# Rotation tables with the norm weights in them, and the rms factor on ScalarE, in a sparse and local attention layer

## The chip, the core and the metric

The kernel runs on one core of a Trainium2 chip. The core has five engines with instruction queues of their own: TensorE (PE in the profile; PEld is its weight load), VectorE (DVE), ScalarE (ACT), GpSimd (POOL) and SyncE (SP, which here only issues DMAs). They meet through semaphores. SBUF is the working memory with 128 partitions, PSUM is where TensorE accumulates. The metric is the device time of one execution in microseconds, lower is better.

## The reference

Four sequences of 1024 tokens with 512 features pass through a layer norm, and then the sum of three things is returned: the input, an attention block and a small product of 8-bit rounded operands. The attention has 16 heads of 128. Queries and local keys are projected, normalized by their root mean square, multiplied by a norm weight for each feature, and half of their features are rotated by an angle that depends on the token:

```python
def rmsnorm(x, w):
    return x * jax.lax.rsqrt(jnp.mean(x * x, axis=-1, keepdims=True) + EPS) * w
...
def apply_rope(x, pos):
    ...
    x1, x2, rest = (x[..., :half], x[..., half:ROPE_DIM], x[..., ROPE_DIM:])
    return jnp.concatenate([x1 * cos - x2 * sin, x1 * sin + x2 * cos, rest], axis=-1)
...
q = apply_rope(rmsnorm(q, qn_w), pos)
...
lk = apply_rope(rmsnorm((hidden_states @ Wlk + blk).reshape(Bq, Sq, NH, D).transpose(0, 2, 1, 3), kn_w), pos)
```

Here `half` is 32 and `ROPE_DIM` 64, so features 64 to 127 are only scaled. Each query then attends in two ways, and the two contexts are averaged: over its own and the previous window of 128 tokens with `lk`, and over the eight best of the compressed entries, one entry for four tokens. The output projection `Wo` follows.

## The kernel before

A chunk is 128 tokens: there are 32, numbered t, eight in each sequence; c is the place of a chunk in its sequence. A unit is one chunk and two heads, so a chunk has eight units u, and there are 256 units n. The number of compressed entries that a chunk sees grows with c, so steps with a large c have wider tiles on TensorE, VectorE and ScalarE.

The order of work is written out by hand: instructions stand on each engine in the order in which the program emits them, and each engine runs its own in that order. The loop over steps s (from L789) works on several units at once. In step s it emits, in this order:

- scores of unit s on TensorE (`scores`, L570 to L581: keys of the previous window, of the own window, compressed keys, mask);
- `keep_context` of unit s - 2 on ScalarE (L733), which moves a finished context out of PSUM;
- `weigh` of unit s: masks, maxima and the eight best on VectorE (L603 to L609), exponentials on ScalarE (L610, L618);
- `queries` of unit s + 2 on TensorE (L443, L444): one PSUM tile `qp` of 128 x 512 with two query heads and two local key heads;
- `settle` of unit s on VectorE (L625 to L636);
- `squares` of unit s + 2 on ScalarE (L294), and `spread` on GpSimd (L288, L289), which makes the factor `r` = 1/rms for each of the four heads;
- `settle_window` of unit s on ScalarE (L641), `to_output` of unit s - 2 on TensorE (L751);
- `turn` of unit s: the probabilities are transposed in 32 x 32 blocks on VectorE (L659) and written to DRAM by SP (L667);
- `values_of` of unit s + 1 on TensorE (L535);
- `normalize` of unit s + 2, the subject of the change;
- `values` of unit s - 1 on TensorE (L718);
- `fetch` of unit s on SP (L701), which reads the probabilities back with the blocks exchanged and so must wait until they have landed;
- `turn_keys` and `fetch_keys` of unit s + 2: block transposes on VectorE (L510, L513) into `thb`, four DMAs to DRAM (L518), two back (L528) into `qT` and `lkT`, all on SP;
- `keep_values` of unit s + 1 on ScalarE (L547).

So keys normalized in step s are used by the scores at the head of step s + 2. Units 0 to 7, and the last one's probabilities, are transposed on TensorE instead (`turn_keys_here`, L488). Beside this run two generators, one that prepares the chunk after next (layer norm and compressed entries) and `chunk_eight`, which rounds the chunk for the 8-bit product with four long GpSimd instructions (L266 to L272) in steps u = 3 and 4, and adds its result in u = 5 (L429).

`normalize` does this for one unit: four VectorE instructions (L465), one for each head, read 128 x 128 of `qp` out of PSUM and multiply by `r` and by the norm weight into `th`. Then `rotate` multiplies the first 64 features of all four heads by the sine on GpSimd (L307, into `rb`) and by the cosine on VectorE (L308, into a spare part of `thb`), and VectorE forms the difference (L309) and the sum (L310) in `th`. `rotate` also serves the compressed keys (`rb_e`, `ra_e`). `th`, `thb` and `rb` have one buffer each; `qp` has two. The table `cs` holds the 32 cosines and 32 sines of each token of a chunk and is loaded two chunks ahead at the end of step u = 6.

Of the kernel before, what the change touches and what calls it, by code (L numbers as in the profile page):

```python
# [12 lines left out]
F32 = mybir.dt.float32  # L13
# [3 lines left out]
ALU = mybir.AluOpType  # L17
AX = mybir.AxisListType

P = 128  # L20
D = 128
RATIO = 4
ROPE = 64
# [15 lines left out]
def kernel(  # L39
# [256 lines left out]
    def rotate(th, cs, nh, a, name):  # L296

        p = th.shape[0]
        a = a.rearrange("p (h t f) -> p h t f", h=nh, t=2)
        bb = work.tile([P, 4, 2, HALF], F32, tag="ropeb", name=f"rb_{name}", bufs=1)  # L300
        bb = bb[:p, 0:nh]
        x12 = th[:, :, 0:ROPE].rearrange("p h (t f) -> p h t f", t=2)

        def wide(v):
            return v.unsqueeze(1).unsqueeze(1).to_broadcast([p, nh, 2, HALF])

        nc.gpsimd.tensor_tensor(bb, x12, wide(cs[:, HALF:ROPE]), ALU.mult)  # L307
        nc.vector.tensor_tensor(a, x12, wide(cs[:, 0:HALF]), ALU.mult)  # L308
        nc.vector.tensor_tensor(x12[:, :, 0, :], a[:, :, 0, :], bb[:, :, 1, :], ALU.subtract)  # L309
        nc.vector.tensor_tensor(x12[:, :, 1, :], a[:, :, 1, :], bb[:, :, 0, :], ALU.add)  # L310
# [144 lines left out]
    def spread(n):  # L455
        w = units[n]
        w["r"] = rstd_of(w["ss"], 4, 1.0 / D, EPS_RMS, f"r_{n}")

    def normalize(n):
        t, u = place(n)  # L460
        w = units[n]
        qp, r = w.pop("qp"), w["r"]
        th = work.tile([P, 4, D], F32, tag="th", name=f"th_{n}", bufs=1)
        for i in range(4):
            nc.vector.scalar_tensor_tensor(  # L465
                th[:, i, :],
                qp[:, ts(i, D)],
                r[:, i : i + 1],
                norm_w[:, i // 2, :],
                ALU.mult,  # L470
                ALU.mult,
            )
        thb = work.tile([P, NB, 2, 2 * BLK], F32, tag="thb", name=f"thb_{n}", bufs=1)
        spare = thb.rearrange("p b t x -> p (b t x)")[:, 0 : 4 * ROPE]
        rotate(th, angles[t][0], 4, spare, f"{n}")
        w["th"], w["thb"] = th, thb

    def by_dma(n):
# [297 lines left out]
    def for_unit(n, *todo):  # L776
        if 0 <= n < NN:
            for f, *more in todo:
                f(n, *more)
# [9 lines left out]
    for s in range(-2, NN + 2):  # L789
# [7 lines left out]
        if u == 4 and 0 <= t and t + 2 < NT:  # L797
            load_x(t + 2, "norm")

        for_unit(s, (scores, 0), (scores, 1))  # L800
        for_unit(s - 2, (keep_context,))
        for_unit(s, (weigh, 0), (weigh, 1))
# [95 lines left out]
```

## Time and profile before

| What | Value |
| --- | --- |
| Median of three runs | 2824.78 us (2822.69 to 2830.02) |
| Profiled execution | 2828.88 us, of which the span from first to last instruction is 2827.2 us |
| Granted TensorE clock in it, mean | 0.997 |
| TensorE busy | 2775.0 us, 98% of the span |
| VectorE busy | 2277.4 us, 81% |
| ScalarE busy | 1302.9 us, 46% |
| GpSimd busy | 818.0 us, 29% |
| L465, 1024 instructions | 282.9 us, 338 ns each |
| L307, 256 | 247.4 us, 966 ns each |
| L308, 256 | 108.8 us, 425 ns each |
| L309 and L310, 256 each | 87.1 and 72.5 us, 340 and 283 ns |
| L733 (PSUM to SBUF, 128 x 128), 512 | 160.4 us, 364 ns each |
| L641 at 128 x 128, 64 | 22.2 us, 393 ns each |

Busy times of one engine's instructions overlap a little when they follow each other, so that four L465 of 338 ns each take 1.12 us together. A busy share says how much an engine had to do, not whether anyone waited for it; for that the starts of its instructions and the table of waits are read. In a timeline, each line gives the start in us from the beginning of the span, the duration, the engine and line, the operation with output and inputs, and in brackets how long the engine was idle before it and what ended that.

### The profile page before, as it was taken

How to read it: one execution, taken by the hardware profiler on the slowest of the kernel's cores; microseconds unless marked ns; L12 is line 12 of the kernel's file. 1: busy time of each engine (PE TensorE's matmuls, PEld its weight loads, DVE VectorE, ACT ScalarE, POOL GpSimd, SP SyncE). 2: the span in 40 equal slices, each digit the busy share in tenths (PEclk: the TensorE clock that was granted, in tenths of full speed). 3: DMA queues.
4: the chain of work that ended last, by engine and by line, in shares of the span. 5: the costliest groups of instructions: out<-in, count | busy, mean ns of one | idle time of the engine just before them, and what ended most of it. 6: DMA issues, size and time to landing. Idle time of an engine off the chain costs nothing. (4 is left out here: it accounts for less than half of the span.)

```text
span 2827.2 us, 48528 instructions
## 1 busy us (share of the span) xinstructions
PE 2775.0 (98%) x12770; PEld 1879.6 (66%) x12969; DVE 2277.4 (81%) x9132; ACT 1302.9 (46%) x5075; POOL 818.0 (29%) x1161
## 2 busy tenths in 40 slices
PE   7999999999999999999999999999999999999998
PEld 4666666666666666666666666666666666666666
DVE  5778888888777888888877788888887777888886
ACT  3444444444444444444444444444444444444443
POOL 3433222222233332232223233222223222322222
PEclk9999999999999999999999999999999999999999
DMA  7344445555444445555544444555554444455553
GB/s 224 93 140 133 137 143 151 147 153 146 133 128 133 138 134 149 148 152 151 148 129 123 137 134 138 150 153 147 149 146 124 134 131 131 136 152 151 149 149 116
DMA packets 620851, 399.85 MB, mean 141 GB/s; under 512 B 306880, under 2 KB 573984, under 8 KB 620576
## 3 DMA queue, kind: packets, MB, share of 16 engines
q1 hardware_dynamic: 608352, 383.18, 47.8%
q10 hardware_dynamic: 12224, 13.56, 1.5%
q8 instruction: 105, 1.72, 0.3%
q14 instruction: 170, 1.39, 0.2%
HBM read 212.53 MB, written 184.03 MB: 140 GB/s over the span
## 5 line engine op out<-in xcount | busy, mean ns | idle before, releaser
L443 PE MATMUL qp<-wqk,xnT 128*128 128x512 f32 x2048 | 944.6, 604 | 4.1 <-DMA scales<-in_L_ffn_scale_dram 3.1
L443 PEld LDWEIGHTS qp<-wqk,xnT 128*128 128x128 f32 x2048 | 370.1, 191 | 383.9 <-issue 370.3
L610 ACT ACTIVATE prob<-sc,neg 128x256 f32<-128x256 f32 (+1 forms) x512 | 236.1, 461 | 786.4 <-DVE taken L609 772.5
L535 PEld LDWEIGHTS vp<-wlv,xnT 128*128 128x128 f32 x2048 | 391.1, 191 | 170.4 <-issue 109.5
L535 PE MATMUL vp<-wlv,xnT 128*128 128x256 f32 x2048 | 488.6, 382 | 6.2 <-DVE lkT L495 2.9
L751 PE MATMUL op<-wo,cT 128*128 128x512 f32 x1024 | 488.0, 599 | 6.0 <-ACT cT L733 1.5
L659 DVE STREAM_TRANSPOSE probB<-prob 128x512 f32<-128x512 f32 (+2 forms) x494 | 282.9, 610 | 79.4 <-ACT prob L641 75.8
L294 ACT ACTIVATE junk<-qp 128x128 bf16<-128x128 f32 x1024 | 284.2, 278 | 100.0 <-remote 56.6
L307 POOL TENSOR_TENSOR rb<-th,cs 128x256 f32<-128x256 f32 x256 | 247.4, 966 | 276.5 <-DVE th L465 276.5
L465 DVE SCALAR_TENSOR_TENSOR th<-qp,r,norm_w 128x128 f32<-128x128 f32 x1024 | 282.9, 338 | 45.1 <-POOL r L289 44.9
L751 PEld LDWEIGHTS op<-wo,cT 128*128 128x128 f32 x1024 | 186.5, 190 | 179.2 <-issue 115.9
L547 ACT COPY lv<-vp 128x256 f32<-128x256 f32 x256 | 95.4, 373 | 449.5 <-PE cp L718 393.5
L288 POOL TENSOR_SCALAR r<-ss 128x4 f32<-128x4 f32 x256 | 49.8, 195 | 862.8 <-ACT junk L294 856.4
L718 PE MATMUL cp<-probT,lv 128*128 128x128 f32 x1920 | 298.3, 275 | 0.7 <-DMA probT<-pr 0.7
L718 PEld LDWEIGHTS cp<-probT,lv 128*128 128x128 f32 x1920 | 275.3, 192 | 14.3 <-PE vp L535 1.1
L289 POOL TENSOR_TENSOR r<-r,nhalf 128x4 f32<-128x4 f32 x256 | 259.9, 1015 | 21.4
L718 PE MATMUL cp<-probT,cv 128*128 128x128 f32 x1536 | 255.6, 275 | 0.0
L580 PE MATMUL sc<-ckT,qT 128*128 128x96 f32 (+7 forms) x1024 | 226.2, 303 | 0.0
L641 ACT ACTIVATE prob<-prob,tot 128x256 f32<-128x256 f32 (+1 forms) x512 | 223.0, 484 | 2.1 <-DVE tot L635 2.0
L309 DVE TENSOR_TENSOR th<-thb,rb 128x128 f32<-128x128 f32 x256 | 87.1, 340 | 158.9 <-POOL rb L307 158.9
L577 PE MATMUL sc<-lkT,qT 128*128 128x128 f32 x1024 | 209.7, 287 | 5.4 <-DMA lkT<-qk 3.9
L718 PEld LDWEIGHTS cp<-probT,cv 128*128 128x128 f32 x1536 | 213.2, 192 | 0.0
(123 smaller groups left out, 4003.8 us busy)
## 6 DMA issues: line engine op xcount, KB each, us to landing
pr<-probB SPq DMA_DIRECT2D x127, 512.0 KB, 2.6
probT<-pr SPq DMA_DIRECT2D x508, 128.0 KB, 2.9
qk<-thb SPq DMA_DIRECT2D x992, 64.0 KB, 2.0
pr<-probB SPq DMA_DIRECT2D x96, 384.0 KB, 2.3
probT<-pr SPq DMA_DIRECT2D x384, 96.0 KB, 2.5
qT<-qk SPq DMA_DIRECT2D x248, 128.0 KB, 2.3
lkT<-qk SPq DMA_DIRECT2D x248, 128.0 KB, 2.5
x_norm<-_attn_hidden_states_dram SPq DMA_DIRECT2D x32, 256.0 KB, 3.1
```

The source lines that it names most:

```text
L289: nc.gpsimd.tensor_tensor(r, r, nhalf[: ss.shape[0], 0:n], ALU.pow)
L294: nc.scalar.activation(junk[: src.shape[0]], src, AF.Square, accum_out=acc)
L307: nc.gpsimd.tensor_tensor(bb, x12, wide(cs[:, HALF:ROPE]), ALU.mult)
L443: nc.tensor.matmul(qp, xnT[:, k, :], wqk_sb[u][:, k, :], start=(k == 0), stop=False)
L465: nc.vector.scalar_tensor_tensor(th[:, i, :], qp[:, ts(i, D)], r[:, i : i + 1], norm_w[:, i // 2, :], ALU.mult, ALU.mult,)
L535: nc.tensor.matmul(vp[:, 0:256], xnT[:, k, :], wlv_sb[u][:, k, :], start=(k == 0), stop=(k == KK - 1),)
L580: nc.tensor.matmul(sc[:, spa], q, ckT[:, 0:m], start=True, stop=False)
L610: nc.scalar.activation(prob[:, loc], sc[:, loc], AF.Exp, bias=neg[:, 0:1], scale=-1.0, accum_out=tot[:, 0:1],)
L641: nc.scalar.mul(prob[:, loc], prob[:, loc], tot[:, 0:1])
L659: nc.vector.transpose(pb[:, :, ds(h * g, g), :], prob[:, parts[0] * P : (parts[-1] + 1) * P].rearrange("p (g b i) -> p b g i", b=NB, i=BLK),)
L718: nc.tensor.matmul(blocks(cp[:, h, :]), v, probT[:, :, h * len(parts) + i - parts[0], :], start=(i == parts[0]), stop=(i == parts[-1]),)
L751: nc.tensor.matmul(op, cT[:, h, :], wo_sb[u][:, h, :], start=(u == 0 and h == 0), stop=(u == NU - 1 and h == 1),)
```

## The change

Per chunk, GpSimd now builds two tables out of the norm weights and the chunk's angles: `cos` (128 x 2 x 128: weight times cosine for the rotated features, the bare weight for the rest) and `sin` (128 x 2 x 2 x 32: weight times sine, with the sign in it). They are built at the head of step u = 6 for the next chunk, with one buffer each, and the sines in `cs` are negated in place for it. Per unit, ScalarE multiplies each head of `qp` by its `r` into `thb`, GpSimd multiplies the two exchanged halves by `sin` in two instructions, and VectorE multiplies everything by `cos` in one and adds the two in another. The compressed keys keep `rotate`.

```diff
+    def make_tables(t):
+        cs, _ = angles[t]
+        cos = work.tile([P, 2, D], F32, tag="cos", name=f"cos_{t}", bufs=1)
+        sin = work.tile([P, 2, 2, HALF], F32, tag="sin", name=f"sin_{t}", bufs=1)
+        halves = norm_w[:, :, 0:ROPE].rearrange("p g (t f) -> p g t f", t=2)
...
+        nc.gpsimd.tensor_tensor(
+            cos[:, :, 0:ROPE].rearrange("p g (t f) -> p g t f", t=2),
+            halves,
+            wide(cs[:, 0:HALF], 2, 2),
+            ALU.mult,
+        )
+        nc.gpsimd.tensor_copy(cos[:, :, ROPE:D], norm_w[:, :, ROPE:D])
+        nc.gpsimd.tensor_tensor(
+            sin[:, :, 1, :], halves[:, :, 0, :], wide(cs[:, HALF:ROPE], 2), ALU.mult
+        )
+        nc.gpsimd.tensor_scalar(cs[:, HALF:ROPE], cs[:, HALF:ROPE], -1.0, None, ALU.mult)
+        nc.gpsimd.tensor_tensor(
+            sin[:, :, 0, :], halves[:, :, 1, :], wide(cs[:, HALF:ROPE], 2), ALU.mult
+        )
+        tables[t] = cos, sin
+
     def normalize(n):
         t, u = place(n)
         w = units[n]
         qp, r = w.pop("qp"), w["r"]
+        cos, sin = tables[t]
         th = work.tile([P, 4, D], F32, tag="th", name=f"th_{n}", bufs=1)
+        thb = work.tile([P, NB, 2, 2 * BLK], F32, tag="thb", name=f"thb_{n}", bufs=1)
+        xr = thb.rearrange("p b t x -> p (b t x)")
         for i in range(4):
-            nc.vector.scalar_tensor_tensor(
-                th[:, i, :],
-                qp[:, ts(i, D)],
-                r[:, i : i + 1],
-                norm_w[:, i // 2, :],
+            nc.scalar.mul(xr[:, ts(i, D)], qp[:, ts(i, D)], r[:, i : i + 1])
+        xr = xr.rearrange("p (g h d) -> p g h d", g=2, h=2)
+        rb = work.tile([P, 2, 2, 2, HALF], F32, tag="ropeb", name=f"rb_{n}", bufs=1)
...
+        for i in range(2):
+            nc.gpsimd.tensor_tensor(
+                rb[:, :, :, i, :],
+                xr[:, :, :, ds((1 - i) * HALF, HALF)],
+                heads_of(sin[:, :, i, :]),
                 ALU.mult,
-                ALU.mult,
-            )
-        thb = work.tile([P, NB, 2, 2 * BLK], F32, tag="thb", name=f"thb_{n}", bufs=1)
-        spare = thb.rearrange("p b t x -> p (b t x)")[:, 0 : 4 * ROPE]
-        rotate(th, angles[t][0], 4, spare, f"{n}")
+            )
+        all_ = th.rearrange("p (g h) d -> p g h d", g=2)
+        nc.vector.tensor_tensor(all_, xr, heads_of(cos), ALU.mult)
+        turned = th[:, :, 0:ROPE]
+        nc.vector.tensor_tensor(
+            turned, turned, rb.rearrange("p g h t f -> p (g h) (t f)"), ALU.add
+        )
         w["th"], w["thb"] = th, thb
...
+        if u == 6 and t + 1 < NT:
+            make_tables(t + 1)
         for_unit(s, (scores, 0), (scores, 1))
```

More of the change, by code (lines that the diff above doesn't have):

```diff
@@ L457, in spread, with wide @@
         w["r"] = rstd_of(w["ss"], 4, 1.0 / D, EPS_RMS, f"r_{n}")
+    tables = {}
+    def make_tables(t):
[3 more added lines that the diff above has]
+        halves = norm_w[:, :, 0:ROPE].rearrange("p g (t f) -> p g t f", t=2)
+        def wide(v, *ones):
+            for _ in ones:
+                v = v.unsqueeze(1)
+            return v.to_broadcast([P, *ones, HALF])
+        nc.gpsimd.tensor_tensor(
[13 more added lines that the diff above has]
+        tables[t] = cos, sin
     def normalize(n):
@@ L462, in normalize, with heads_of @@
         qp, r = w.pop("qp"), w["r"]
+        cos, sin = tables[t]
         th = work.tile([P, 4, D], F32, tag="th", name=f"th_{n}", bufs=1)
+        thb = work.tile([P, NB, 2, 2 * BLK], F32, tag="thb", name=f"thb_{n}", bufs=1)
+        xr = thb.rearrange("p b t x -> p (b t x)")
         for i in range(4):
-            nc.vector.scalar_tensor_tensor(
-                th[:, i, :],
-                qp[:, ts(i, D)],
-                r[:, i : i + 1],
-                norm_w[:, i // 2, :],
-                ALU.mult,
+            nc.scalar.mul(xr[:, ts(i, D)], qp[:, ts(i, D)], r[:, i : i + 1])
+        xr = xr.rearrange("p (g h d) -> p g h d", g=2, h=2)
+        rb = work.tile([P, 2, 2, 2, HALF], F32, tag="ropeb", name=f"rb_{n}", bufs=1)
+        def heads_of(v):
+            return v.unsqueeze(2).to_broadcast([P, 2, 2, v.shape[-1]])
+        for i in range(2):
[3 more added lines that the diff above has]
+                heads_of(sin[:, :, i, :]),
                 ALU.mult,
             )
-        thb = work.tile([P, NB, 2, 2 * BLK], F32, tag="thb", name=f"thb_{n}", bufs=1)
-        spare = thb.rearrange("p b t x -> p (b t x)")[:, 0 : 4 * ROPE]
-        rotate(th, angles[t][0], 4, spare, f"{n}")
+        all_ = th.rearrange("p (g h) d -> p g h d", g=2)
[4 more added lines that the diff above has]
+        )
         w["th"], w["thb"] = th, thb
```

## The prediction

> **What bounds the kernel now.** I read the page's shares first, then the spacing of TensorE's matmuls, then who TensorE waited for, and last the path from `r` to the keys, which is the only path through the edited code that TensorE waits on.
>
> ```profile
> span 2827.2 us, 48528 instructions
> ...
> PE 2775.0 (98%) x12770; PEld 1879.6 (66%) x12969; DVE 2277.4 (81%) x9132; ACT 1302.9 (46%) x5075; POOL 818.0 (29%) x1161
> ```
>
> 98% on PE can mislead, because matmul ends are modelled. So I took the starts of the matmul records instead. In the timeline a 512-column float32 pass of the query product (L443) starts 429 ns after the one before, a 256-column pass (L535) 216 ns, a 128-column pass of L718 112 ns, without gaps. The time from one unit's first query matmul to the next is a fixed pattern: for chunks 2, 10, 18 and 26 (the same place c = 2 in each batch) the eight steps read 9.96, 10.38, 10.01, 10.45, 11.75, 10.01, 10.76, 10.87 us, and all but one of the 32 agree within 0.1 us. An engine that waits on others does not repeat like that. Adding only the starts that come over 150 ns later than the usual spacing gives 42.2 us lost: about 23 us before 81 us, 7 us after 2800 us, the other 12 in some 25 short waits between. That is all a lighter VectorE could return.
>
> In the table of waits the ones that hold TensorE's matmuls (waiter, awaited, us in total, times, longest) are small:
>
> ```profile
> PE sc L577 <- DMA lkT<-qk: 3.9, 8, 1.2
> ...
> PE tq L488 <- DVE th L310: 3.2, 1, 3.2
> ...
> PE vp L535 <- DVE lkT L495: 2.9, 2, 2.1
> ...
> PE sc L570 <- DMA qT<-qk: 2.0, 3, 1.4
> ```
>
> Only the first and the last recur: keys that come back late from DRAM. The chain of waits at the end runs through VectorE, but that is where a chain goes when TensorE has no gap to follow; its step length in chunk 31 (10.81 to 11.29 us) is TensorE's own.
>
> The path of one unit's keys, from the timeline (start, us, engine, line; unit 137):
>
> ```profile
> 1507.00 1.02 POOL L289 TENSOR_TENSOR r<-r,nhalf 128x4 f32<-128x4 f32 x1
> ...
> 1508.05 1.12 DVE L465 SCALAR_TENSOR_TENSOR th<-qp,r,norm_w 128x128 f32<-128x128 f32 x4 [0.98 <-POOL r L289]
> ...
> 1509.21 0.42 DVE L308 TENSOR_TENSOR thb<-th,cs 128x256 f32<-128x256 f32 x1
> ...
> 1509.26 0.97 POOL L307 TENSOR_TENSOR rb<-th,cs 128x256 f32<-128x256 f32 x1 [1.24 <-DVE th L465]
> ...
> 1510.26 0.29 DVE L309 TENSOR_TENSOR th<-thb,rb 128x128 f32<-128x128 f32 x1 [0.62 <-POOL rb L307]
> ...
> 1510.47 0.28 DVE L310 TENSOR_TENSOR th<-thb,rb 128x128 f32<-128x128 f32 x1
> ...
> 1510.79 0.45 DVE L510 STREAM_TRANSPOSE thb<-th 128x256 f32<-128x256 f32 x1
> ...
> 1511.15 0.40 DVE L513 STREAM_TRANSPOSE thb<-th 128x256 f32<-128x256 f32 x1
> ...
> 1511.75 1.82 SPq L518 DMA_DIRECT2D qk<-thb  x4
> ...
> 1515.06 0.38 SPq L528 DMA_DIRECT2D qT<-qk  x1
> ...
> 1515.48 0.51 SPq L528 DMA_DIRECT2D lkT<-qk  x1
> ...
> 1518.37 0.40 PE L570 MATMUL sc<-lkT,qT 128*128 128x128 f32 x2
> ```
>
> Two reserves lie in it. The first, the cover, is the time between the end of L513 and the first issue of L518, in which SP still waits for the probabilities to land before it may fetch them (L701): here 0.20 us, over all 248 such units 1.10 us in the median, under 0.4 us for 29. The second, the slack: from the issue of the `lkT` fetch to the first score matmul there are 3.61 us in the median, and about 2.1 us where the matmul really waited; so about 1.5 us is slack.
>
> [...]L307 takes 0.97 us when L308 (0.42) started 0.05 us ahead of it, and 0.90 us in the one case (36.12 us) where 0.32 us of L308 was left. Either way the rest is about 0.58 us[...]. [...]L641 at 128 elements measures 393, L733 out of PSUM 364.
>
> **The change part by part, for one unit.**
> *Removed from VectorE:* four L465 (1.12 us together), L308 (0.42), L309 and L310 (0.53 from the first start to L510): 2.07 us. *Added:* one 512-element table product, 0.69 us[...], and one 256-element sum, 0.43: 1.12 us. VectorE is 0.95 us freer per unit, some 240 us over 256 units. On the path to the end this is worth 0, since TensorE's stream hides it.
> *ScalarE:* four multiplications out of PSUM, [...]1.18 us. They stand behind `settle_window` (L641), and behind them wait the `lv` copy (L547), the context (L733) and the next exponentials (L610). In the unit above they would run 1508.1 to 1509.3, so L547 ends near 1509.7 (1508.5 before) and L733 near 1510.3 (1509.7 before); L610 follows at 1512.70, and the output matmul that needs the context at 1514.03. Hidden. If `r` were later by over 2.4 us it would not be; where it is latest (c = 7, u = 5, r 5.07 us after the last query matmul) L733 would end about 7.3 us after it, and L610 starts about 8.5 us after it.
> *GpSimd:* one 256-element product becomes two of 128. The 64-element row (L307 on 32 partitions, 0.310, of which 0.106 beside VectorE) and 0.58 for 256 give about 0.34 each: 0.68. [...]I take them one after the other: 0.69 + 0.68.
> *From `r` to the first transpose:* before 1508.02 to 1510.79 = 2.77 us. After: 0.05 to start, 1.18, 0.08 to the next engine, 1.37, 0.03, 0.43 = 3.14 us, later by about 0.4. Lower end -0.3 (if they run side by side, 0.68 drops out), upper end +1.0 (products at 0.6 us each, as for a mostly fixed cost). I take +0.4[...]. Laid over every unit's cover and slack, +0.4 gives 0 to 0.7 us of new waiting in the whole run, +1.0 gives 1.5 to 6.6, -0.3 nothing, as what is late next is the landing of the probabilities on SP. In chunks with c above 4, VectorE itself started late (r to the end of L513 3.74 us against 3.54), so there the path grows by 0.2 only.
> *Tables:* five GpSimd instructions per chunk at the head of the step u = 6, by the same line about 0.33 + 0.3 + 0.2 + 0.2 + 0.2 = 1.2 us, 32 times. GpSimd then stands idle for over 5 us before the next `r`, in nearly every chunk (L288 waited 856 us in 180 times). They may push one sum per chunk back by up to 1.2 us; that is unit u = 7, with cover 0.7 to 1.8 us: 0, and if uncovered at most a few tenths in the first chunks of a batch.
> *The wait at L443:* the changed program no longer waits for VectorE ahead of the first query matmul (214 units had that wait). Worth nothing: 34 units lack it already, and they show the same spacing. Unit 137 has it, 138 lacks it; both weight loads come 0.54 us apart, then 0.43:
>
> ```profile
> 1500.39 0.30 PEld L443 LDWEIGHTS qp<-wqk,xnT 128*128 128x128 f32 x2
> 1500.93 0.19 PEld L443 LDWEIGHTS qp<-wqk,xnT 128*128 128x128 f32 x1 [0.24 <-issue]
> ...
> 1510.27 0.30 PEld L443 LDWEIGHTS qp<-wqk,xnT 128*128 128x128 f32 x2
> 1510.81 0.19 PEld L443 LDWEIGHTS qp<-wqk,xnT 128*128 128x128 f32 x1 [0.24 <-issue]
> ```
>
> *Start:* unit 0's keys are turned on TensorE, which waited 3.2 us for L310: +0.4. At 34 us the `lv` copy now stands behind four multiplications and holds the transpose L410 about 1 us longer, but TensorE loses 2.1 us soon after waiting for `lkT`, which comes no later; absorbed. *End:* the last unit's transposes were done at 2797.3 and its L518 issued at 2798.93: covered.
>
> **Sum.** 0.4 at the start + 0 to 0.7 in the middle = about +1 us on the profiled execution's 2828.88 (span 2827.2 and 1.7 around it). That execution lies 4.1 us above the median of the runs, 2824.78; on the median's scale: 2826 us.
>
> **Rivals.**
> 1. *VectorE sets the pace where it is busiest* (c = 5 to 7, 96 units): -0.95 x 96 = -91, 2734 us. For it: 81% busy and the chain. Against: the repeated steps. 3%.
> 2. *The wait at L443 costs its 83 ns* (512 against 429 ns): 214 x 0.083 = 17.8, 2807 us. Against: the 34 units. 3%.
> 3. *The short waits vanish*: with the 12 us between 81 and 2800 us gone, 2814 us. Against: those I followed sit behind SP's wait for the probabilities. 5%.
> 4. *Slower: the keys arrive late.* Place: L518 to L528, units with cover under 0.4 us and the short steps of c = 0 and 1. Price: at +1.3 us on the path, 5 to 15 us, 2835 us. It decides from about +1.0, that is with GpSimd's products near 0.6 us each or the tables in front of the sums more often than once per chunk. 12%.
> 5. *ScalarE blocked on `r`* so that exponentials slip and then the probabilities: 0.3 us on each of 32 steps, +10, 2835 us. 3%.
> Forecast as worked out: 74%.
>
> **How the numbers follow.** No change is what lies within 0.3%, 8.5 us, about what a measurement of this kernel can tell. Faster: rivals 1 and 2, over half of 3, and 1% from the forecast's own spread: 10%. Slower: most of 4 and 5 and 2% of the forecast: 13%. Same: 77%. The range takes in rivals 3 and 4 and the 7 us that three runs of one kernel spread over: 2815 to 2837.
>
> **What would show it.** VectorE busy near 1950 us, ScalarE near 1670, TensorE's step pattern of c = 2 unchanged to 0.1 us; the gap from 512 to 429 ns still there; r to the end of the transposes near 3.95 us; the cover shorter by 0.4. Wrong it would be if the eight steps of a chunk all shortened (rival 1 or 2), or if waits of `sc` for `lkT<-qk` went from 8 to some 40 (rival 4).

## The result, and the profile after

The changed kernel takes 2840.17 us in the median of five runs (2837.87 to 2847.13), the kernel before, beside it, 2824.83 us. The ratio is 1.0056, with a 95% interval from 1.0039 to 1.0074: slower by 15.3 us. The forecast was 2826, its range ended at 2837. The profiled execution of the changed kernel took 2847.13 us (span 2845.4, against 2827.2 before); it is the slowest of the five, 7 us above the median one.

The page of the changed kernel, span and busy time of each engine:

```profile
span 2845.4 us, 49374 instructions
...
PE 2793.1 (98%) x12969; PEld 1880.4 (66%) x12969; DVE 2063.8 (73%) x7852; ACT 1551.3 (55%) x6099; POOL 979.4 (34%) x1577
```

VectorE is 214 us less busy and the kernel is slower. So the lost time is looked for where it was looked for before: in the starts of TensorE's matmuls that come over 150 ns later than their usual spacing. Before, they add up to 42.0 us (23.7 at the start, 11.5 in the middle, 6.9 at the end), after to 59.6 (23.9, 28.6, 7.1). These 17.6 us are nearly the whole 18.2 us between the two spans, and they all lie in the middle: scores that wait for keys rose from 11.5 us at 24 places to 25.3 us at 37, and 3.4 us are matmuls at a lower granted clock (0.50; windows in the last section). The table of TensorE's waits after (waiter, awaited, us in total, times, longest) shows the same pair as before, grown:

```profile
PE sc L612 <- DMA qT<-qk: 6.6, 6, 1.6
PE sc L619 <- DMA lkT<-qk: 4.7, 15, 0.6
...
PE tq L530 <- DVE th L515: 3.0, 1, 3.0
```

These rows hold only a part of the 25.3 us, because the table puts many of the same waits down to ScalarE instructions. Of the 37 places, 29 have the landing of their key fetch on record, and in each of them the matmul starts 0.04 to 0.27 us after it. So it is the keys that the scores wait for.

The keys' own path did what the forecast said. The timeline of the changed kernel, again unit 137 (start, us, engine, line), from the last exponentials and squares ahead of `r` to the issue of the key stores:

```profile
1515.50 0.38 PE L444 MATMUL qp<-bias_b,sel 128*128 128x512 bf16 x1
...
1515.93 0.28 ACT L660 ACTIVATE prob<-sc,neg 128x32 f32<-128x32 f32 x1
1516.10 0.28 ACT L294 ACTIVATE junk<-qp 128x128 bf16<-128x128 f32 x1
...
1518.03 0.19 POOL L288 TENSOR_SCALAR lnr<-lnst 128x1 f32<-128x1 f32 x1 [5.51 <-DVE ckT L412]
1518.30 0.55 POOL L289 TENSOR_TENSOR lnr<-lnr,nhalf 128x1 f32<-128x1 f32 x1
...
1519.21 1.02 POOL L289 TENSOR_TENSOR r<-r,nhalf 128x4 f32<-128x4 f32 x1
...
1520.26 1.14 ACT L498 ACTIVATE thb<-qp,r 128x128 f32<-128x128 f32 x4 [2.02 <-POOL r L289]
...
1521.43 0.69 DVE L513 TENSOR_TENSOR th<-thb,cos 128x512 f32<-128x512 f32 x1 [2.67 <-ACT thb L498]
1521.48 1.38 POOL L506 TENSOR_TENSOR rb<-thb,sin 128x128 f32<-128x128 f32 x2 [1.25 <-ACT thb L498]
...
1522.89 0.42 DVE L515 TENSOR_TENSOR th<-th,rb 128x256 f32<-128x256 f32 x1 [0.76 <-POOL rb L506]
1523.35 0.45 DVE L552 STREAM_TRANSPOSE thb<-th 128x256 f32<-128x256 f32 x1
1523.72 0.40 DVE L555 STREAM_TRANSPOSE thb<-th 128x256 f32<-128x256 f32 x1
...
1524.18 1.76 SPq L560 DMA_DIRECT2D qk<-thb  x4
```

From the end of `r` (1520.23) to the first transpose there are 3.12 us; 3.14 were forecast. What the forecast did not look at stands above `r`. In the kernel before, the same unit's squares did not follow the exponentials at once; there is a pause between them, which the trace calls only `remote`, and they start as long after the last query matmul as in any unit that is not late:

```profile
1503.72 0.28 ACT L618 ACTIVATE prob<-sc,neg 128x32 f32<-128x32 f32 x1
1504.41 0.28 ACT L294 ACTIVATE junk<-qp 128x128 bf16<-128x128 f32 x1 [0.41 <-remote]
```

After, the squares start when ScalarE is done with the exponentials, without a gap. Where the squares start like this, `r` hangs on the unit before it. There is a ring, with one round for each step: squares of unit n (ScalarE), `r` (GpSimd), products and transposes (the change), then `weigh` of the unit before n, which stands behind those transposes on VectorE (L645 to L651), its exponentials, and behind them on ScalarE the squares of unit n + 1. A step of TensorE that is longer than this ring lets lateness go; a shorter one passes it on and adds to it. All of it by the place u of the unit, worked out from the records (means in us over the units from 12 on; ring: 1.48 for the squares, the time from there to the end of the second transpose, and from there to the end of the exponentials; late: from the start of the query product's last float32 pass, L443, plus 0.64 us, to the start of the squares, where 0.2 to 0.3 is the least that occurs; keys turned: from that same point to the end of the second transpose, in the median; times from the last query matmul, further down, are counted from that point too):

| u | 0 | 1 | 2 | 3 | 4 | 5 | 6 | 7 |
|---|---|---|---|---|---|---|---|---|
| step before | 10.38 | 10.67 | 10.33 | 10.73 | 12.01 | 10.31 | 11.20 | 11.28 |
| step after | 10.47 | 10.83 | 10.55 | 10.87 | 11.98 | 10.31 | 11.27 | 11.24 |
| ring before | 9.95 | 10.66 | 9.97 | 10.55 | 11.30 | 11.77 | 9.92 | 9.92 |
| ring after | 10.46 | 11.38 | 10.21 | 10.20 | 11.06 | 12.00 | 10.18 | 10.41 |
| squares late before | 0.28 | 0.28 | 0.35 | 0.30 | 0.27 | 0.27 | 1.61 | 1.12 |
| squares late after | 0.52 | 0.52 | 1.06 | 0.70 | 0.30 | 0.21 | 1.76 | 1.37 |
| keys turned before | 6.94 | 7.58 | 6.96 | 7.52 | 8.31 | 8.76 | 8.22 | 7.76 |
| keys turned after | 7.59 | 8.45 | 7.94 | 7.51 | 7.83 | 8.82 | 8.63 | 8.48 |

At u = 5 the ring is longer than the step in both kernels, and the squares of u = 6 come late. Before, the steps of u = 6 and 7 were 1.3 us longer than the ring, and by u = 0 the lateness was gone. (At u = 7 some 0.7 us of it are new in both kernels: ScalarE squares the compressed keys between the exponentials and the unit's squares.) After, it lasts to u = 3, because the ring at u = 0 and 1 is now as long as the step or longer. The rows add up: at u = 1 after, 0.52 + 11.38 - 10.83 = 1.07 us should be left for u = 2, and 1.06 is there. The keys of u = 0, 1 and 2 are turned 0.65, 0.87 and 0.98 us later, though the path from `r` grew by 0.35 us at most. The time of the steps above the shortest one of the same place (c and u) in the two runs, summed over chunks 1 to 30, grew from 16.1 to 35.1 us, and the steps u = 1 to 3 hold most of it: 1.1 us before, 17.3 after.

Two links are not as simple as this list has them. First, at u = 0, 1 and 5 `r` is mostly released not by the squares but by background work ahead of it on GpSimd: after the change the compressed entries' product in 26 of 30 units of u = 0, `lnr` of the layer norm in 28 of 30 of u = 1, the rounding product L266 in all 31 of u = 5. Unit 137 above is such a one: GpSimd stood idle for 5.51 us until VectorE's L412, which comes behind `weigh` and `settle`, then made `lnr`, and only then `r`. So there the ring closes from VectorE to GpSimd without the squares. Of the 0.72 us that the ring grew by at u = 1, 0.38 lie between the squares and `r` and 0.34 behind it.

Second, a key store is often not released by the transposes. SP has to fetch the probabilities first, and they come from the same late exponentials. In the changed kernel 11 of the 37 waits (8.0 of the 25.3 us) are of units whose stores were issued less than 0.4 us after the transposes, before the change 2 of 24; in the others the turned keys lay ready while SP waited for the probabilities. These were stored 0.34, 0.40 and 0.71 us later at u = 0, 1 and 2, and `lkT` was fetched 0.48, 0.69 and 0.78 us later (means). The lateness thus reaches TensorE in two ways; what each cost was not separated. The place does fit: units of u = 0 to 2 have 11.2 us of the waits, and had 0.8 before.

### The profile page after: what moved, and what is told of

Its sections match the earlier page's. It is cut to its first block, busy times and chain, and to the rows that moved or that the text cites. A ratio compares the mean times of both kernels' runs of the same rounds, so it can differ in the third digit from the quotient of the medians.

```text
span 2845.4 us, 49374 instructions
## 1 busy us (share of the span) xinstructions
PE 2793.1 (98%) x12969; PEld 1880.4 (66%) x12969; DVE 2063.8 (73%) x7852; ACT 1551.3 (55%) x6099; POOL 979.4 (34%) x1577
## 3 DMA queue, kind: packets, MB, share of 16 engines
q14 instruction: 174, 1.43, 0.2%
## 4 chain that ended last, share of the span: by engine, by line
PE 57%; DVE 14%; POOL 9%; ACT 7%; DMA 6%; issue 3%; SPq 2%; ACTq 0%; POOLq 0%; DVEq 0%
PE qp L443 19%; PE op L793 9%; PE vp L577 8%; PE cp L760 8%; POOL rb L506 4%; PE sc L622 3%; PE sc L619 3%; PE sc L612 3%; ACT junk L294 2%; POOL r L289 2%; DVE sc L645 2%; DVE top L648 2%; DMA lkT<-qk 2%; ACT thb L498 2%; DVE taken L651 2%
## 5 line engine op out<-in xcount | busy, mean ns | idle before, releaser
L443 PE MATMUL qp<-wqk,xnT 128*128 128x512 f32 x2048 | 947.7, 606 | 4.5 <-ACT xnT L343 2.9
L443 PEld LDWEIGHTS qp<-wqk,xnT 128*128 128x128 f32 x2048 | 371.7, 192 | 386.1 <-issue 372.6
L506 POOL TENSOR_TENSOR rb<-thb,sin 128x128 f32<-128x128 f32 x512 | 352.3, 707 | 222.7 <-ACT thb L498 220.8
L498 ACT ACTIVATE thb<-qp,r 128x128 f32<-128x128 f32 x1024 | 291.9, 368 | 224.1 <-POOL r L289 220.3
L513 DVE TENSOR_TENSOR th<-thb,cos 128x512 f32<-128x512 f32 x256 | 177.8, 694 | 293.7 <-ACT thb L498 293.2
L760 PE MATMUL cp<-probT,lv 128*128 128x128 f32 x1920 | 297.8, 275 | 1.0 <-DMA probT<-pr 1.0
L760 PEld LDWEIGHTS cp<-probT,lv 128*128 128x128 f32 x1920 | 274.8, 192 | 14.5 <-PE vp L577 1.4
L515 DVE TENSOR_TENSOR th<-th,rb 128x256 f32<-128x256 f32 x256 | 128.5, 502 | 194.6 <-POOL rb L506 194.6
L760 PE MATMUL cp<-probT,cv 128*128 128x128 f32 x1536 | 255.4, 275 | 0.0
L760 PEld LDWEIGHTS cp<-probT,cv 128*128 128x128 f32 x1536 | 212.9, 192 | 0.0
```

The lines of the kernel that those rows point to most:

```text
L443: nc.tensor.matmul(qp, xnT[:, k, :], wqk_sb[u][:, k, :], start=(k == 0), stop=False)
L498: nc.scalar.mul(xr[:, ts(i, D)], qp[:, ts(i, D)], r[:, i : i + 1])
L506: nc.gpsimd.tensor_tensor(rb[:, :, :, i, :], xr[:, :, :, ds((1 - i) * HALF, HALF)], heads_of(sin[:, :, i, :]), ALU.mult,)
L760: nc.tensor.matmul(blocks(cp[:, h, :]), v, probT[:, :, h * len(parts) + i - parts[0], :], start=(i == parts[0]), stop=(i == parts[-1]),)
```

## The experiments

Thirteen kernels were run, each timed in five rounds beside the kernel before (2825 to 2828 us), so ratios are compared. "Late" is the mean lateness of the squares over all units, "waits" what the scores lose in the middle in one profiled execution.

| kernel | ratio to before, 95% | late | waits (places) |
|---|---|---|---|
| before | 1 | 0.55 | 11.5 (24) |
| after | 1.0056 (1.0039 to 1.0074) | 0.80 | 25.3 (37) |
| one table | 1.0047 (1.0035 to 1.0060) | 0.80 | 19.0 (35) |
| ScalarE's multiplications alone | 1.0001 (0.9993 to 1.0009) | 0.46 | 7.7 (16) |
| path longer | 1.0015 (1.0005 to 1.0025) | 0.72 | 15.1 (29) |
| weigh later | 1.0082 (1.0068 to 1.0096) | 1.09 | 25.8 (42) |
| multiplications of `qp` as well | 1.1149 (1.1134 to 1.1164) | 3.24 | 234.7 (276) |
| product out of PSUM | 0.9976 (0.9967 to 0.9985) | 0.35 | 6.4 (13) |
| raw halves | 0.9979 (0.9972 to 0.9986) | 0.39 | 8.3 (15) |
| `r` in two halves | 1.0119 (1.0105 to 1.0133) | 1.07 | 33.2 (55) |
| after, background work later | 1.0109 (1.0095 to 1.0123) | 0.54 | 34.4 (57) |
| PSUM product, background work later | 1.0033 (1.0021 to 1.0046) | 0.28 | 19.4 (35) |
| before, background work later | 1.0043 (1.0029 to 1.0057) | 0.48 | 19.9 (30) |
| after, rounding later | 1.0031 (1.0019 to 1.0042) | 0.86 | 12.3 (21) |
| PSUM product, rounding later | 0.9974 (0.9963 to 0.9984) | 0.39 | 6.5 (10) |

The waits of one execution are good to some 4 us at best: the run with ScalarE's multiplications alone has the time of the kernel before and 3.8 us less of them. The recorded expectations call the ring a loop.

**Are the tables the cost?**

```diff
-        cos, sin = tables[t]
+        cos, sin = tables[0]
...
-        if u == 6 and t + 1 < NT:
-            make_tables(t + 1)
+        if s == -2:
+            make_tables(0)
```

> The changed kernel with its two tables built once, from chunk 0, and used for all 32 chunks; so the rotation of the other chunks is computed with the wrong angles, and 31 of the 32 table builds are left out. Theory A (a loop of one step: r, products, transposes, weigh on VectorE, exponentials and the next squares on ScalarE, next r, has become longer than TensorE's short steps): the tables are no link of it, 0 to -4 us against the changed kernel, that is about 2836 to 2840; scores waiting for keys stay near 25 us. Rival B (the tables, 1.9 us of GpSimd ahead of the sums and products of one unit in eight, cost the time): -12 to -18 us, back to about 2825, keys waits near 10 us.

The ratio is 1.0047 beside 1.0056, with intervals that overlap. The five table instructions take 465 + 485 + 316 + 300 + 319 ns, 1.89 us for each chunk, but their price is at most a few us of the 15. (The waits of its one profiled execution, 19.0 us, are fewer than the 25 expected.) Rival B falls.

**Is it ScalarE's work and its wait for `r`?** Two kernels asked it. The first, out of the kernel before:

```diff
+        spill = work.tile([P, D], F32, tag="spill", name=f"spill_{n}", bufs=1)
+        for i in range(4):
+            nc.scalar.mul(spill, qp[:, ts(i, D)], r[:, i : i + 1])
```

> The kernel before with the four ScalarE multiplications by r out of PSUM that the change adds, at the change's place in ScalarE's order, but into a tile that nobody reads: ScalarE has the change's new work and its new wait for r, VectorE and GpSimd work as before. Rival C (ScalarE blocked on r delays the values copy, the context and the next exponentials): +8 to +16 us. Theory A (loop; the exponentials come over 3 us later, so ScalarE is free again by then): 0 to +2 us, last query matmul to r unchanged at 3.80.

It was slower by 325 us, which neither theory had. The timeline of this kernel shows why:

```profile
1517.07 1.01 POOL L289 TENSOR_TENSOR r<-r,nhalf 128x4 f32<-128x4 f32 x1
...
1518.12 1.57 ACT L466 ACTIVATE spill<-qp,r 128x128 f32<-128x128 f32 x4
...
1519.80 1.13 DVE L468 SCALAR_TENSOR_TENSOR th<-qp,r,norm_w 128x128 f32<-128x128 f32 x4 [1.35 <-ACT spill L466]
```

and so does its table of waits:

```profile
DVE th L468 <- ACT spill L466: 270.8, 162, 4.0
```

VectorE reads nothing that ScalarE writes here, yet it waits for it, 270.8 us in 162 times, and in the unit shown it starts 0.11 us after ScalarE's last one: both read `qp`, and in this program the second reader of that PSUM tile waits for the first. So `r` to the end of the transposes grew from 3.54 to 5.22 us, the ring from 10.51 to 12.13 us in the mean, and the mean step from 10.87 to 12.13. The ring had become the pace of the whole kernel. The run does not answer what it was made for, but it shows the ring at full strength. The second kernel multiplies the norm weights instead of `qp`:

```diff
+            nc.scalar.mul(spill, norm_w[:, i // 2, :], r[:, i : i + 1])
```

> The kernel before with four ScalarE multiplications by r at the change's place in ScalarE's order, but of the norm weights in SBUF into a tile that nobody reads, so that VectorE's products have no reason to wait for them: ScalarE has the change's work and its wait for r, nothing else changes. Rival C: +8 to +16 us. Loop theory: 0 to +3 us, r to the end of the transposes 3.54 us and last query matmul to r 3.8 to 3.9 us.

It has the ratio 1.0001. ScalarE's new work and its wait for `r` cost nothing by themselves. Rival C falls, and the forecast's "hidden" was right.

**Is it each unit's own path, or the ring?** Both kernels are the kernel before with one more VectorE instruction in each unit, a block transpose of a constant tile.

```diff
+    def linger():
+        nc.vector.transpose(
+            fill[:, 1, :].rearrange("p (b i) -> p b i", i=BLK),
+            fill[:, 0, :].rearrange("p (b i) -> p b i", i=BLK),
+        )
...
+        linger()
         nc.vector.transpose(
             thb[:, :, 0, :].rearrange("p b (i g) -> p b i g", g=2), th[:, :, 0:2, :]
         )
```

> The kernel before with one more VectorE instruction of about 0.35 us (a block transpose of 192 columns of a constant tile) just ahead of the two key transposes; nothing else. The path from r to the transposes and the loop both grow by 0.35, as in the change, while ScalarE and GpSimd do exactly what they did. Theory A (loop): +8 to +18 us over the kernel before, waits of the scores for keys from 12 to about 25 us, last query matmul to r up by about 0.3 us. Rival C (the price comes from ScalarE's four multiplications or GpSimd's products standing before other work): under 2 us. Theory D (only the direct path, each unit's own keys 0.35 us later, as the prediction had it): under 2 us, and the time from the last query matmul to r unchanged at 3.80.

The filler takes 0.37 us but fell partly into the time that the transpose waits for the sums anyway: the path grew by 0.14 us only (3.54 to 3.68). The time grew by 4.2 us (interval 1.4 to 7.1), between the figures of the two theories, which had been reckoned for 0.35. But the last query matmul to `r` went from 3.80 to 4.04 us, which the direct path alone can't do. The second puts the filler behind the unit's transposes:

```diff
     def weigh(n, h):
...
+        if h == 0:
+            linger()
```

> The kernel before with the same extra VectorE instruction of about 0.35 us, now at the head of weigh, behind the key transposes of the unit two ahead in VectorE's order. A unit's own way from r to its keys is untouched; the loop over weigh, exponentials and the next squares grows by 0.35. Theory A (loop): +5 to +14 us, last query matmul to r up by about 0.3 us, r to the end of the transposes unchanged at 3.54 in the median. Theory D (direct path only): under 2 us. Rival C: under 2 us.

TensorE's waits for keys in this kernel, the two rows that were 2.0 us (3 times) and 3.9 us (8 times) before:

```profile
PE sc L579 <- DMA qT<-qk: 9.5, 11, 1.5
PE sc L586 <- DMA lkT<-qk: 7.0, 15, 1.1
```

`r` to the end of the transposes stays at 3.54 us in chunks with c under 4 and 3.74 above, as before. From there to the end of the exponentials it takes 0.26 us more at every place. The whole ring grows by 0.34 us in the mean, since at u = 0, 1 and 5 `r` also stands longer behind GpSimd's background work. The time grows by 23 us: more than the change cost, with nothing added between a unit's `r` and its keys. The last query matmul to `r` goes from 3.80 to 4.47 us. Theory D, the forecast's, allowed under 2 us; the ring theory's upper end, 14 us, was too low as well. The filler also stands ahead of the probabilities that SP waits for, so a part of the price may be this direct delay; no run separates it. But one pass of the filler can't give what is seen: the squares of u = 2 are 1.20 us late and not 0.35, which is 0.85 more, so lateness was handed on.

**Can the change be kept and the ring shortened?** VectorE takes its product out of PSUM again, now with the table; ScalarE multiplies only the rotated columns:

```diff
-            nc.scalar.mul(xr[:, ts(i, D)], qp[:, ts(i, D)], r[:, i : i + 1])
+            nc.scalar.mul(xr[:, i, :], qp[:, ds(i * D, ROPE)], r[:, i : i + 1])
...
+        for i in range(4):
+            nc.vector.scalar_tensor_tensor(
+                th[:, i, :],
+                qp[:, ts(i, D)],
+                r[:, i : i + 1],
+                cos[:, i // 2, :],
+                ALU.mult,
+                ALU.mult,
+            )
...
-        nc.vector.tensor_tensor(all_, xr, heads_of(cos), ALU.mult)
```

> The changed kernel with the table product taken by VectorE straight out of PSUM, (qp x r) x cos in four instructions as before the change; ScalarE multiplies only the 64 rotated columns of each head by r, for GpSimd's two products. If VectorE and ScalarE read qp at the same time, r to the first key transpose is about 2.5 us (before 2.77, after 3.12) and the loop theory expects the time of the kernel before or a little less, 2818 to 2828. If VectorE's products wait until ScalarE's multiplications are done, as they did in the run with ScalarE's extra multiplications, that stretch is about 2.9 us, between before and after: 2830 to 2838, waits of the scores for keys 14 to 22 us. Rival C (ScalarE's multiplications standing before the values copy and the context cost the time): ScalarE's new work is hardly less, so it stays near 2838 to 2842.

It beats both kernels: ratio 0.9976, 7 us under the kernel before. Its timeline:

```profile
1513.05 1.01 POOL L289 TENSOR_TENSOR r<-r,nhalf 128x4 f32<-128x4 f32 x1
1514.09 0.93 ACT L499 ACTIVATE thb<-qp,r 128x64 f32<-128x64 f32 x4 [0.61 <-POOL r L289]
...
1515.10 0.87 POOL L516 TENSOR_TENSOR rb<-thb,sin 128x128 f32<-128x128 f32 x2 [1.04 <-ACT thb L499]
1515.12 1.13 DVE L507 SCALAR_TENSOR_TENSOR th<-qp,r,cos 128x128 f32<-128x128 f32 x4 [0.97 <-issue]
...
1516.35 0.42 DVE L523 TENSOR_TENSOR th<-th,rb 128x256 f32<-128x256 f32 x1
1516.81 0.45 DVE L560 STREAM_TRANSPOSE thb<-th 128x256 f32<-128x256 f32 x1
```

VectorE did wait for ScalarE's multiplications (134.4 us in 132 times), the second of the two cases expected, so `r` (to 1514.06) to the first transpose takes 2.75 us and not 2.5; the time went below that case's 2830 to 2838 all the same. What the expectation left out is GpSimd. Its products now run beside VectorE's, which read only one large operand from SBUF. The two kernels' records of that instruction (duration in ns: least, median, most), first after, then this kernel:

```profile
L506 POOL TENSOR_TENSOR rb<-thb,sin x512: 442/680/972, 24.8 to 2816.1; 128x128 f32<-128x128 f32 x171
```

```profile
L516 POOL TENSOR_TENSOR rb<-thb,sin x512: 443/455/472, 24.5 to 2786.0; 128x128 f32<-128x128 f32 x171
```

The first row mixes the two products of a pair. In the changed kernel's records the first of them, which starts 45 ns after the table product, takes 964 ns, and the second, which starts after the table product has ended, 450 (medians over 256 units). So beside this VectorE instruction with two large SBUF operands a GpSimd product took 514 ns longer than behind it; beside the one with a PSUM operand it took 455 ns in all. It did not stand still beside the first, though: in unit 137 the table product ran to 1522.12 us, and GpSimd's two products, which take 0.87 us in the kernel with the PSUM product, were done at 1522.86 and not at 1522.99. At u = 3, 4 and 5 the squares to the turned keys take 5.02, 5.76 and 6.37 us, where the kernel before took 5.71, 6.47 and 6.94; elsewhere they move by less than 0.2. So the squares at u = 6 are 0.98 us late and not 1.61, and by u = 0 that is gone. Whether GpSimd's shorter products alone shortened those three places was not tried.

In the next kernel GpSimd's products no longer need `r`: ScalarE copies the unscaled halves, and VectorE multiplies by `r` twice. They still stand behind `r` in GpSimd's order, so they do not run while it is computed, although the expectation says so.

```diff
+        nc.scalar.copy(xr, qp.rearrange("p (k d) -> p k d", d=D)[:, :, 0:ROPE])
...
+        rot = rb.rearrange("p g h t f -> p (g h) (t f)")
+        for i in range(4):
+            nc.vector.scalar_tensor_tensor(
+                th[:, i, 0:ROPE],
+                rot[:, i, :],
+                r[:, i : i + 1],
+                th[:, i, 0:ROPE],
+                ALU.mult,
+                ALU.add,
+            )
```

> As the run before this one, but ScalarE's multiplications by r are gone: it copies the unscaled rotated columns out of PSUM in one instruction that does not wait for r, GpSimd multiplies them by sin while r is computed, and VectorE multiplies by r in its four products out of PSUM and again in four 64-column multiply-adds. r to the first key transpose about 2.1 to 2.3 us (before 2.77). Loop theory: the loop is 0.5 us shorter than before the change, last query matmul to r falls below 3.8 us, waits of the scores for keys fall below 11 us, time 2812 to 2824. If the cost of the change lay in the tables or in GpSimd's two products: 2835 to 2842, since both stay.

Ratio 0.9979, 2819.84 us, in the range expected. The path was not as expected: `r` to the first transpose takes 2.86 us in the median and not 2.1 to 2.3; it is shorter, 1.9 to 2.1, only at u = 0 to 2. The mean ring fell to 10.06 us, 0.45 under that of before, and gave no more than the kernel above with 10.31. It was shortened where it was no longer than the step already (at u = 1 from 10.62 to 9.59 us), and at u = 5, where it is longer than the step, it takes 11.43 us and not 11.21. That fits the ring: it costs only where it is longer than the step.

Both kernels keep the tables and GpSimd's two products, so neither of these by itself was the cost of the change. What both take away is the product that VectorE took from SBUF, behind all of ScalarE's multiplications and beside GpSimd. How much of the cost was the waiting, how much GpSimd's longer products and how much ScalarE's wider multiplications was not separated.

**Another link of the ring: `r`.** The changed kernel with `r` for two heads as soon as their squares are there:

```diff
-        for_unit(s + 2, (squares, (0, 1, 2, 3)), (spread,))
+        for_unit(
+            s + 2, (squares, (0, 1)), (spread, 0), (squares, (2, 3)), (spread, 1)
+        )
```

> The changed kernel with r computed in two halves, one for two heads as soon as their squares are summed; the rest is the change, its four ScalarE multiplications, its two GpSimd products and its tables included. ScalarE can multiply the first two heads while GpSimd works on the second half, so the last of the four multiplications ends about 0.9 us earlier after the squares. Loop theory: the change's cost goes, 2818 to 2830, waits of the scores for keys 11 us or less. Rivals B and C (tables; ScalarE's multiplications ahead of other work)[...]: all of that is untouched, so 2836 to 2844.

A clear miss: 33 us slower than before, 18 us more than the change cost. By u, the squares to the turned keys did fall where GpSimd has nothing else (u = 2 from 5.36 to 4.87 us, u = 6 from 5.36 to 5.20), and by less than the 0.9 expected; they rose at u = 5 from 7.18 to 7.73, at u = 0 from 5.64 to 5.86, at u = 1 from 6.54 to 6.75. The timeline of unit 149 (u = 5) in this kernel:

```profile
1651.88 1.27 POOL L266 TENSOR_TENSOR qv_x<-qv_x,qm_x 128x512 f32<-128x512 f32 x1 [6.86 <-DVE row L376]
...
1653.51 0.70 POOL L289 TENSOR_TENSOR r<-r,nhalf 128x2 f32<-128x2 f32 x1
...
1654.56 0.70 POOL L289 TENSOR_TENSOR r<-r,nhalf 128x2 f32<-128x2 f32 x1
1655.22 1.27 POOL L268 TENSOR_TENSOR qv_x<-qv_x,qm_x 128x512 f32<-128x512 f32 x1
...
1656.45 1.31 POOL L506 TENSOR_TENSOR rb<-thb,sin 128x128 f32<-128x128 f32 x2
```

GpSimd runs two rounding products of 1.27 us around `r`. In this unit `r` in one piece takes 1.02 us, in two pieces twice 0.70, so the second half, and with it L268 and the two products, come later. The ring got longer exactly where it already was longer than the step, and the squares at u = 6 are 2.33 us late. The mean ring (10.75 us) is that of the change; a mean over places does not show what a ring costs.

**Moving the rounding out of the ring.** One line moved puts the background work of a step behind `r`, in the changed kernel, in the kernel with the PSUM product and in the kernel before:

```diff
-        steps()
         for_unit(s + 2, (squares, (0, 1, 2, 3)), (spread,))
+        steps()
```

> The changed kernel with one line moved: the first of the two calls in a step that emit the background work (the rounding of activations and weights, the next chunk's layer norm) now stands behind the squares and r instead of ahead of them. GpSimd's 1.27 us rounding product then no longer stands in front of r at u = 5, and ScalarE's copies for the next chunk no longer stand in front of the squares. Nothing of the change itself is touched. Loop theory: from the end of the squares to the end of the key transposes at u = 5 falls from 7.18 to about 5.9 us, the squares of the next unit start up to 1 us earlier, waits of the scores for keys fall from 25 to 12 us or less, time 2820 to 2830. If instead each unit simply pays for its own later keys, without carrying it over to the next unit, only one unit in eight gains: 2834 to 2840.

> The same line moved in the kernel that takes the table product out of PSUM on VectorE (2820 us). Loop theory: the squares of the units after u = 5 start earlier here too (1.0 us late before this edit), the 6.4 us of score waits in the middle fall to 2 to 5 us: 2814 to 2820. More is not there to be had, since some 28 us of TensorE's loss lie at the start and the end.

> The same line moved in the kernel before the change. Loop theory: the squares of the units after u = 5 start up to 1 us earlier (1.61 us late before), the 11.5 us of score waits in the middle fall to 4 to 7 us: 2816 to 2822. If the waits in the middle come from something else than late r (the landing of the probabilities on the queue that also stores the keys), nothing changes: 2823 to 2827.

All three came out 12 to 16 us slower than without the move. The squares did start earlier (u = 6 in the changed kernel 1.21 us late and not 1.76; at u = 5 7.18 fell to 6.61 and not to 5.9). But in the changed kernel the fetch of the keys of u = 0 was now issued 14.08 us after their queries, and not 12.40, and some 22 us of its waits are of that place (in the other two it came after 13.37 and 13.41 us, and not 11.80 and 11.92). The timeline of unit 136 (u = 0) in the first of the three shows where that came from:

```profile
1515.75 1.04 POOL L289 TENSOR_TENSOR r<-r,nhalf 128x4 f32<-128x4 f32 x1
1516.76 0.31 POOL L307 TENSOR_TENSOR rb_e<-kv,cse 32x64 f32<-32x64 f32 x1
...
1517.11 0.18 DVE L309 TENSOR_TENSOR kv<-ra_e,rb_e 32x32 f32<-32x32 f32 x1 [1.78 <-POOL rb_e L307]
...
1517.32 0.75 DVE L701 STREAM_TRANSPOSE probB<-prob 128x256 f32<-128x256 f32 x2
1518.10 0.34 SPq L709 DMA_DIRECT2D pr<-probB  x1
```

The compressed entries' product (L307) stands behind `r` too now; VectorE waits 1.78 us for it, with the transposes of the probabilities behind it, and SP, which has to fetch those probabilities before it may store the keys, waits as well: the key stores are issued 2.4 us after the transposes in this place, where it was 0.8. One link was shortened and another chain into the same queue lengthened. So the move was made once more, only in the step that rounds:

```diff
-        steps()
+        if u != 3:
+            steps()
         for_unit(s + 2, (squares, (0, 1, 2, 3)), (spread,))
+        if u == 3:
+            steps()
```

> The changed kernel with the background work emitted behind the squares and r in one step of eight only, u = 3, where it holds the rounding products of unit u = 5. In the run that moved it in all steps, squares to keys at u = 5 took 6.61 us instead of 7.18, but at u = 0 the keys were issued 1.7 us later, behind late probabilities. Loop theory with that explanation: 6.6 us at u = 5, the squares after it start about 0.55 us earlier (u = 6: 1.76 to 1.2 us late), the time from the squares to the issue of the keys at u = 0 as in the changed kernel, waits of the scores for keys from 25 to 12 to 18 us, time 2826 to 2835. If the loop theory is wrong: 2838 us or more.

> The same in the kernel with the table product out of PSUM (2820 us before this edit). Loop theory: the squares after u = 5 start some 0.2 us earlier (6.37 to 6.16 us at u = 5, as in the run that moved all steps), of 6.4 us of score waits 2 to 5 stay: 2815 to 2820. If the loop theory is wrong: 2820 us or more.

The changed kernel goes from ratio 1.0056 to 1.0031 (2835.79 us, just above what was expected); the second delay is gone (fetch after 12.21 us at u = 0), though the two intervals overlap a little. The direction is the ring's, but not the amount at the place named: u = 5 fell only to 7.04 us, since both rounding products now stand between `r` and GpSimd's products, and the squares at u = 6 are still 1.64 us late. That part of the expectation failed. The mean lateness even rose, from 0.80 to 0.86 us, while the waits halved; why is open. The mean lateness of the squares is thus no measure of the cost by itself. With the PSUM product the move brings nothing that can be told apart, 0.9974 after 0.9976, and u = 5 went up, from 6.37 to 6.55 us, where a fall to 6.16 was expected.

## Why the prediction was wrong

Right were the bound (TensorE's stream) and most costs of single pieces. The step pattern of c = 2 held for 29 of the 32 steps: chunk 2 still reads 9.96, 10.38, 10.01, 10.45, 11.75, 10.01, 10.76 us, but its eighth step takes 11.52 us and not 10.87, and chunks 18 and 26 have one longer step each (11.33 for 10.38, 11.70 for 10.01). The path from `r` was put at 3.14 us and is 3.12; to the end of the transposes 3.89 us in the median against 3.95. In the chunks with large c it grew by 0.15, where 0.2 was said. ScalarE's multiplications were put at 1.18 us, hidden, and are 1.14, hidden (by L733 in the kernel before, 0.367 us for one and 0.63 for two in a row, they would be 1.16). The table product was put at 0.69 us and takes 0.69, as L760 of as many elements does in the kernel before. The wait at L443 was put at nothing: the weight loads come 0.54 us apart without it too. The start changed by 0.2 us, the end by 0.2.

Some terms were off without weight. The tables take 1.89 us and not 1.2. GpSimd's small products were put at 0.34 us each; the second of a pair, behind the table product, takes 0.45. That they and the table product run strictly one after the other was the author's assumption, on which the +0.4 rested, and no trace shows it. The sum of 0.69 + 0.68, 1.37, still came out near the 1.43 us measured from the table product's start, by luck: each product is longer than was said, but the first one, of 0.96 us, starts beside VectorE's. VectorE is busy 2064 us and not 1950; the prediction's own 240 us less would have made it 2037. ScalarE is busy 1551 us and not 1670.

The step that failed is this one: "Laid over every unit's cover and slack, +0.4 gives 0 to 0.7 us of new waiting in the whole run". It held the moment of `r`, and that of the probabilities' landing, fixed in every unit, and asked of each one alone whether its 0.4 us fits. But `r` itself moved: from the last query matmul to `r` there are 4.10 us in the mean, where there were 3.80. The exponentials ahead of the squares now end 0.58 us after the queries and not 0.19 in the mean, because `weigh` stands behind the transposes that came later. The probabilities, which follow from them, are stored up to 0.71 us later. In place of 0 to 0.7 us of new waiting there were 13.8 us (11.5 to 25.3), and 3.4 us at a lower clock. At u = 2 the keys are turned 0.98 us later, at u = 1 0.87: near the +1.0 from which the prediction itself reckoned with the slower case. Rival 4 had the right wait (`sc` for keys, 8 times before, 15 after in the table of waits, not the 40 that were said) and nearly the right price, but another mechanism and place: it asked for slow GpSimd products and named the short steps of c = 0 and 1. In chunks 1 to 30 the steps of c = 4 lost most, 7.9 us; those of c = 0 lost 4.4 and those of c = 1 only 0.2.

The prediction had a hint in hand. It found that VectorE starts late in chunks with c above 4, and that `r` comes as late as 5.07 us after the last query matmul at u = 5. What makes `r` late there is the rounding product L266 ahead of it on GpSimd, not the squares. Asking what stands behind this late `r` would have led to the transposes, the exponentials and the squares of u = 6, already 1.61 us late in the kernel before.

## What to carry to other kernels

When an instruction on a path gets later by 0.4 us, ask what stands behind it on its in-order engine, and follow that until it comes back to the start of the path: if it does, compare the time around with each step, not with the mean, because lateness that a short step can't let go of is handed on. Slack that was measured in the old kernel holds for a delay that ends with its unit, not for one that the next unit inherits. Moving work off a busy engine can lengthen such a ring although that engine does less. And a ring is worth shortening only at the places where it is longer than the step: a mean over all places does not show them.

## What the runs showed of the hardware

At two places in the middle of the changed kernel's execution waits of TensorE were followed by a lower granted clock. Three windows of the changed kernel (stretch, length, busy us of PE, PEld, DVE, ACT and POOL with instructions, clock, DMA share, GB/s):

```profile
1066.00:1068.00 2.00, 1.02 (x6) 0.86 (x7) 1.10 (x2) 0.90 (x4) 1.37 (x2) 1.00 0.73 252
1068.00:1070.00 2.00, 2.00 (x12) 1.46 (x11) 1.90 (x10) 0.00 (x0) 0.00 (x0) 0.71 0.18 52
1070.00:1072.00 2.00, 2.00 (x4) 0.90 (x3) 1.83 (x11) 1.53 (x6) 0.00 (x0) 0.50 0.74 205
```

Two waits of 1.39 and 0.67 us end at 1066.5 and 1067.5 us, and from some 1.4 us later the granted clock is 0.50 for about 3.4 us: the eight float32 passes of L443 at 1068.89 us take 5.35 us, where eight without this take 3.68. At the other place the waits are 1.38 and 0.53 us, and the clock falls 0.3 us ahead of the eight passes, which take 5.20. The two are worth 3.4 us. Other waits were not followed by this, among them single ones of 1.91 us (at 1492 us) and 1.79 us (at 1789 us), with a granted clock of 1.00 in the 7 us after each, so the length of a wait does not decide it by itself; what does was not tried. In the kernel that multiplied `qp` as well, with 0.9 us of score waits in a step, the mean granted clock of the profiled execution was 0.975, and 0.997 in the kernel before. So at the two places above the 2.06 and 1.91 us of waits were followed by some 1.7 us of loss each. GpSimd's power instruction took 0.55 us for one column, 0.70 for two and 1.02 for four, so that two halves cost more than the whole.
